# Block sums of a graph layer turned by transposing matmuls, and six buffers of gathered rows instead of seven

## The chip, the cores and the metric

The kernel runs on one core of one Trainium2 chip. A core has five instruction streams that matter here: TensorE (PE in the profile; its loads of stationary operands are listed as PEld), VectorE (DVE), ScalarE (ACT), GpSimd (POOL), and SyncE (SP), beside the queues that carry transfers. The metric is device microseconds from launch to end; lower is better. Three runs of the kernel before gave 4693.23, 4697.88 and 4697.90 us, with a median of 4697.88 us. All arithmetic is float32.

## What is computed

The reference is one message passing layer over a graph of 12500 nodes with 160 features each (64 scalars, and 32 vectors of three components) and 400000 edges, sorted by the node that they end in. Cut to what matters:

```python
h_s = s @ lin1_ws * a / sqrt(64);  h_v = (v @ lin1_wv) * a / sqrt(32)   # per node
w1, w2, w3, w4, w5 = split(silu(edge_scalars @ fc_w1 / 8) @ fc_w2 / 8)  # per edge, 224 wide
es, ev = h_s[src], h_v[src]                                             # gathered rows
e0, e1 = edge_attr[:, :1], edge_attr[:, 1:4]
m_s1 = w1 * es * e0;            m_s2 = w4 * einsum(ev, e1) / 3
m_v1 = (w2 * es) x e1;          m_v2 = w3 * ev * e0
m_v3 = w5 * cross(ev, e1) / 2
agg = segment_sum(concat(m_s1, m_s2), concat(m_v1, m_v2, m_v3); dst) / 4
o = (agg @ lin2) * a            # per node
pre = sc + o                    # sc = (x @ sc_w) * a, the self connection
g = concat(silu(pre_s[:64]), sigmoid(pre_s[64:96]) * pre_v)
out = layernorm(x + g)
```

## The kernel before, in words

**Tiles, steps and blocks.** The edges are cut into 3125 tiles of 128, one edge to a partition. A step handles four tiles, so there are 782 steps; the main loop runs over them and writes the instructions of every engine in the order in which they stand in the program. Nothing reorders them later. Three tiles in a row are a block; two blocks make a pair, and the tiles of a step alternate between the two blocks' places. Since the edges are sorted, the edges of a block end in a window of at most 16 nodes in a row.

**One step.** `gather` (L471) issues four indirect transfers on POOL's queue, one for each tile; each fetches 128 rows of 160 values from a table `h_tab` of node features into a buffer `hg`. These buffers come from the pool `deep`. The third of a step's four gathers has an extra wait, called the pace: it does not start before the last `weights` matmul of three steps earlier is done. `weights` (L546) makes the 224 edge weights of each of the four tiles on PE, into one of two PSUM buffers `pw`. DVE then makes a one-hot matrix of edge against window node (`one_hot`, L609, into a free part of `pw`), the products of weights and gathered rows (`products`, L556 and three times L564) and `sel`, the one-hot matrix times the four edge attributes (L618). Two steps later `sum_up` has PE add up the tiles of a block with `sel` as the stationary operand (L625, into PSUM buffer `pa`): 64 rows (four attributes times 16 nodes) by 416 columns of products for each of the pair's two blocks.

**What a pair's sums go through.** `close` copies a finished `pa` to SBUF as `sa` (ACT, L853): 128 partitions, of which the index is block, attribute, node. `turned` (L641) brings this onto the other axis for two pairs at a time: products on partitions, attribute and node on columns. For each of the four groups of 128 product columns it multiplies a slice of `sa` by those columns of the unit matrix `ident` that select the wanted attributes (three attributes, 96 columns, for two groups; one attribute, 32 columns, for the other two), into a PSUM buffer of the kind `misc`; ACT copies the result into `tt` (L644). When eight pairs or so have gathered in `tt`, `second` multiplies by the second linear map (L654), ACT copies that to `os` (L657), and DVE adds each block's window into the accumulator `acc` of all nodes (L662). One step's hidden layer (L462 on PE, L464 on ACT) is made for every two steps, also through `misc`, of which there are two buffers.

**The nodes' end.** `finish` handles four tiles of 128 nodes at a time: `turn` makes, for a tile's scalars and vectors, the self connection (L709) and then adds the turned piece of `acc` behind it by a product with `ident` (L711), both into one `misc` buffer; tanh, gate, layer norm and the store (L714 to L756) follow.

**What sets the order.** The loop gives each half of a step at most one of the odd jobs: a hidden layer, a turn of sums, a second map, a turn of nodes (`spread_out`). In the last steps the order follows what is ready. DVE, ACT and POOL wait for PE through semaphores; two `pw`, two `pa` and two `misc` buffers and the pool `deep` bound how far one engine runs ahead of another.

A matmul instruction of float32 operands shows as two records in the profile, each with a weight load of its own.

Of the kernel before, what the change touches and what calls it, by code (L numbers as in the profile page):

```python
# [10 lines left out]
F32 = mybir.dt.float32  # L11
# [10 lines left out]
P = 128  # L22
S = 64
V = 32
V3 = 3 * V
# [6 lines left out]
W = 16  # L32
# [17 lines left out]
NPR = 2 * S + 3 * V3  # L50
ROWS = 4 * W
# [10 lines left out]
def gnn_kernel(  # L62
# [21 lines left out]
    nc = tc.nc  # L84
# [10 lines left out]
    consts = ctx.enter_context(tc.tile_pool(name="consts", bufs=1))  # L95
# [111 lines left out]

    ident = consts.tile([P, P], F32, name="ident")
    make_identity(nc, ident)
    iota_i = consts.tile([P, W], I32, name="iota_i")  # L210
    nc.gpsimd.iota(iota_i, pattern=[[1, W]], base=0, channel_multiplier=0)
    eps = consts.tile([P, 1], F32, name="eps")
# [415 lines left out]

    def turned(psum, sas, tt, b, n):

        pt = psum.tile([P, 8, 4, W], F32, name="pt", tag="misc")
        k = n * ROWS
        wanted = ident.rearrange("p (b k w) -> p k b w", b=2, k=4)[:k]
        for m, sa in enumerate(sas):
            plane = 0
            for four in range(4):
                c = min(four * P, NPR - P)
                of = slice(1, 4) if four < 2 else slice(0, 1)
                planes = slice(plane, plane + of.stop - of.start)
                plane = planes.stop  # L640
                nc.tensor.matmul(pt[:, planes, m * n:(m + 1) * n], sa[:k, c:c + P],  # L641
                                 wanted[:, of, :n], start=True, stop=True)
        n *= len(sas)
        nc.scalar.copy(tt[:, :, b:b + n], pt[:, :, :n])  # L644

    def second(pool, psum, tt, nb):
        po = psum.tile([V3, 2, NO, W], F32, name="po", tag="misc")
        for k, to in enumerate("sv"):
            of = [key for key in terms if key[0] == to]
            for n, (_, part, four) in enumerate(of):  # L650
                assert part and four < 2 or not part and four >= 2
                r = slice(P - V if four == 3 else 0, P)
                a = tt[r, four * 3 + part - 1 if part else 4 + four]
                nc.tensor.matmul(po[:, k, :nb], l2[r, terms[to, part, four]], a[:, :nb],  # L654
                                 start=(n == 0), stop=(n == len(of) - 1))
        os = pool.tile([V3, 2, NO, W], F32, name="os", bufs=1)
        nc.scalar.copy(os[:, :, :nb], po[:, :, :nb])  # L657
        return os
# [21 lines left out]
    def finish(fin, psum, t0, nt, p, most=NF, pool=None):  # L680
# [17 lines left out]
        def turn(ks, away=False):  # L698
            if not held:
                held.extend(fin.tile([P, most, *shape], F32, name=name) for name, shape in (  # L700
                    ("g", [V3]), ("y", [D]), ("st", [6]), ("mv", [2]), ("rs", [])))
            g, y = held[:2]
            pp = psum.tile([P, 2, 2, V3], F32, name="pp", tag="misc")
            for k in ks:
                c = (t0 + k) * P
                for m in range(2):
                    if connect:
                        w, a = ((scs, xs), (scv, xv))[m]
                        nc.tensor.matmul(pp[:, k % 2, m], a[:, k * P:(k + 1) * P], w,  # L709
                                         start=True, stop=False)  # L710
                    nc.tensor.matmul(pp[:, k % 2, m], acc[:, m, c:c + P], ident[:V3, :V3],  # L711
                                     start=not connect, stop=True)
            for k in ks:
                nc.scalar.activation(g[:, k], pp[:, k % 2, 0], AF.Tanh, scale=half_at[:, t0 + k:t0 + k + 1])  # L714

            n = len(ks)
            if away:
                pc = fin.tile([P, 2, 2, V3], F32, name="pc", bufs=2)
                nc.scalar.copy(pc[:, :n], pp[:, :n])
                pp = pc  # L720

            def gate():
                k = slice(ks[0], ks[0] + n)
                nc.vector.scalar_tensor_tensor(y[:, k, :S], g[:, k, :S], 1.0, pp[:, :n, 0, :S],
                                               op0=OP.add, op1=OP.mult)
                for k in ks:
                    nc.vector.scalar_tensor_tensor(
                        y[:, k, S:].rearrange("p (c i) -> p i c", i=3),
                        g[:, k, None, S:].to_broadcast([P, 3, V]), 1.0,
                        pp[:, k % 2, 1].rearrange("p (i c) -> p i c", i=3),  # L730
                        op0=OP.add, op1=OP.mult)
                for k in ks:
                    nc.vector.scalar_tensor_tensor(y[:, k], y[:, k], half_at[:, t0 + k:t0 + k + 1],
                                                   xt[:, k], op0=OP.mult, op1=OP.add)

            return gate
# [33 lines left out]
    with tc.tile_pool(  # L770
# [3 lines left out]
    ) as mine, tc.tile_pool(  # L774
        name="late", bufs=2
    ) as late, tc.tile_pool(name="edge", bufs=2) as edge, tc.tile_pool(
        name="deep", bufs=7
    ) as deep, tc.tile_pool(name="banks", bufs=1, space=PSUM) as banks:
        pw_ps = Banks(banks, "pw", Q * 256, 2)
        pa_ps = Banks(banks, "pa", 512, 2)  # L780
# [416 lines left out]
```

## Time and profile before

| what | value |
|---|---|
| median of three runs | 4697.88 us |
| the profiled execution | 4732.17 us |
| its span, first to last instruction | 4730.4 us |
| mean granted TensorE clock | 0.88 |
| PE busy | 4056.1 us (86%), 19977 records |
| POOL busy | 2986.1 us (63%), of which gathers 2955.4 us |
| DVE busy | 2369.7 us (50%) |
| ACT busy | 840.1 us (18%) |
| bytes moved | 412.54 MB, 87 GB/s on average |

The profiled execution is 34 us (0.7%) longer than the median; differences are to be read within one execution. Busy shares are averages over the whole span. An idle time in the profile stands in square brackets behind the instruction that ended it, with the name of what released it; "issue" is idle time that no recorded event explains, and "remote" is a release that the profile could not put down to an instruction just then ending (the page's name for it is "another core or an unknown queue"; here there is only one core). "x4" behind a row counts records that were put together.

### The profile page before, as it was taken

To read this page: it belongs to the slowest core of one execution; us is meant where nothing else is said; L and a number is where in the kernel's file an instruction comes from. 1 tells how busy PE (TensorE), PEld (TensorE's weight loads), DVE (VectorE), ACT (ScalarE), POOL (GpSimd) and SP (SyncE) were. 2 spreads that over 40 slices of the span, in tenths; PEclk is the share of its full clock that TensorE was granted. 3 is DMA by queue.
4 is the path that set the end of the run, shared out by engine and by line. 5 is a ranking of instruction groups with operands and counts; after the bars stand their busy time and mean duration, and the time that the engine had idled before them with its cause. 6 is when DMAs were issued, how large, how long until landed. Compare 5 with 4: busy or idle time off the path is not lost.

```text
span 4730.4 us, 57897 instructions
## 1 busy us (share of the span) xinstructions
PE 4056.1 (86%) x19977; PEld 2153.1 (46%) x19977; DVE 2369.7 (50%) x6410; ACT 840.1 (18%) x1872; POOL 2986.1 (63%) x3172
## 2 busy tenths in 40 slices
PE   5888888888888898888888888888888888888887
PEld 3444444444444444444444444444444444444444
DVE  5544554545544445545455455454554545545454
ACT  1211111111111111111211111111111111111112
POOL 5666666666666666666666666666666666666663
PEclk8888898988998888898898898888898889888898
DMA  6333333333333333333333333333333333333331
GB/s 204 92 77 78 94 86 78 93 78 85 94 77 86 86 84 87 85 85 84 88 85 84 88 85 84 88 85 78 93 85 78 93 77 87 94 77 87 88 83 46
DMA packets 237527, 412.54 MB, mean 87 GB/s; under 512 B 78040, under 2 KB 160961, under 8 KB 237093
## 3 DMA queue, kind: packets, MB, share of 16 engines
q0 software_dynamic: 152960, 266.64, 21.5%
q1 hardware_dynamic: 83668, 141.96, 12.4%
q8 instruction: 160, 2.62, 0.2%
q14 instruction: 145, 1.19, 0.1%
q10 hardware_dynamic: 594, 0.13, 0.0%
HBM read 392.49 MB, written 16.00 MB: 86 GB/s over the span
## 4 chain that ended last, share of the span: by engine, by line
PE 55%; DVE 15%; another core or an unknown queue 14%; issue 11%; POOL 3%; DMA 2%; ACT 0%; DVEq 0%; SPq 0%; POOLq 0%; ACTq 0%
PE pa L625 20%; PE pw L546 13%; DVE pr L564 8%; PE misc L641 7%; PE misc L462 6%; PE misc L654 6%; POOL hg L471 3%; DVE sel L618 2%; PE misc L711 2%; DVE pr L556 1%; PE misc L709 1%; DVE pw L609 1%; DVE acc L662 1%; DMA hg<-h_tab,idx 1%
## 5 line engine op out<-in xcount | busy, mean ns | idle before, releaser
L471 POOL DMA_INDIRECT hg<-h_tab,idx x3125 | 2955.4, 946 | 1682.1 <-issue 823.6
L625 PE MATMUL pa<-pr,sel 128*64 128x416 f32 x6250 | 1610.4, 593 | 167.5 <-issue 164.2
L609 DVE TENSOR_TENSOR pw<-rel,iota 128x64 f32<-128x64 int16 x782 | 179.1, 229 | 2199.7 <-remote 1374.9
L564 DVE TENSOR_TENSOR pr<-pw,hg 128x384 f32<-128x384 f32 x2346 | 1152.2, 546 | 0.0
L546 PE MATMUL pw<-w,hid 64*128 64x224 f32 x6250 | 954.4, 407 | 171.6 <-issue 66.4
L546 PEld LDWEIGHTS pw<-w,hid 64*128 64x128 f32 x6250 | 609.0, 205 | 818.5 <-issue 536.8
L625 PEld LDWEIGHTS pa<-pr,sel 128*64 128x64 f32 x6250 | 447.8, 149 | 1047.0 <-issue 1011.3
L641 PE MATMUL misc<-ident,sa 128*128 128x96 f32 (+1 forms) x4168 | 613.2, 297 | 111.5 <-issue 107.6
L641 PEld LDWEIGHTS misc<-ident,sa 128*128 128x128 f32 x4168 | 568.8, 213 | 203.1 <-issue 196.6
L556 DVE TENSOR_TENSOR pr<-pw,hg 128x512 f32<-128x512 f32 x782 | 540.0, 691 | 29.1 <-DVE pw L609 1.5
L462 PE MATMUL misc<-es,w 128*128 128x512 f32 (+1 forms) x784 | 464.2, 672 | 38.7 <-DVE rel L424 19.6
L644 ACT COPY tt<-misc 128x512 f32<-128x512 f32 (+1 forms) x263 | 152.9, 581 | 1697.8 <-remote 982.8
L464 ACT ACTIVATE hid<-misc 128x512 f32<-128x512 f32 x392 | 234.9, 599 | 916.8 <-remote 469.8
L853 ACT COPY sa<-pa 128x416 f32<-128x416 f32 x521 | 263.6, 506 | 548.8 <-PE pw L546 207.4
L654 PE MATMUL misc<-tt,l 128*96 128x256 f32 (+5 forms) x1496 | 357.9, 386 | 3.2 <-issue 2.6
L618 DVE TENSOR_TENSOR sel<-pw,eas 128x256 f32<-128x256 f32 x782 | 321.5, 411 | 0.1
L654 PEld LDWEIGHTS misc<-tt,l 128*96 128x96 f32 (+1 forms) x1496 | 224.4, 165 | 131.0 <-issue 72.9
L662 DVE TENSOR_TENSOR acc<-acc,os 96x32 f32 x1042 | 193.5, 186 | 83.5 <-PE misc L711 32.4
L711 PE MATMUL misc<-ident,acc 96*128 96x96 f32 x392 | 116.6, 393 | 135.5 <-DVE acc L662 118.3
L462 PEld LDWEIGHTS misc<-es,w 128*128 128x128 f32 x784 | 124.3, 198 | 163.5 <-issue 147.0
L711 PEld LDWEIGHTS misc<-ident,acc 96*128 96x128 f32 x392 | 87.2, 276 | 152.0 <-DVE acc L662 124.1
L657 ACT COPY os<-misc 96x512 f32<-96x512 f32 (+2 forms) x68 | 38.3, 563 | 477.4 <-PE pw L546 134.3
(93 smaller groups left out, 695.2 us busy)
## 6 DMA issues: line engine op xcount, KB each, us to landing
es<-in_es_t_dram SPq DMA_DIRECT2D x258, 384.0 KB
hg<-h_tab,idx POOLq DMA_INDIRECT x3125
h_tab<-ht POOLq DMA_DIRECT2D x24, 320.0 KB
xt<-in_x_dram SPq DMA_DIRECT2D x23, 320.0 KB
out_dram<-y SPq DMA_DIRECT2D x23, 320.0 KB
xv<-in_xv_t_dram SPq DMA_DIRECT2D x23, 192.0 KB
eat<-in_ea_dram SPq DMA_DIRECT2D x41, 96.0 KB
xw<-in_xs_t_dram SPq DMA_DIRECT2D x6, 512.0 KB
```

The costliest lines, as they stand in the source:

```text
L462: nc.tensor.matmul(ph[:k, c], w1[:k, :k], es[:k, t0 * P + c0 * P:t0 * P + c1 * P], start=True, stop=True)
L471: got = nc.gpsimd.indirect_dma_start(out=hg[:, t, :], out_offset=None, in_=h_tab, in_offset=bass.IndirectOffsetOnAxis(ap=i, axis=0))
L546: weighed.append(nc.tensor.matmul(pw[:, t, :NWT], hid[r, c * P:(c + 1) * P], w2[r], start=True, stop=True).ins.name)
L556: nc.vector.tensor_mul(two, pw[:, :n, :2 * S].rearrange("p t (k c) -> p t k c", k=2), hg[:, :n, None, :S].to_broadcast([P, n, 2, S]))
L564: nc.vector.tensor_mul(pr[:, :n, first:first + V3].rearrange("p t (i c) -> p t i c", i=3), pw[:, :n, None, 2 * S + k * V:2 * S + (k + 1) * ...
L618: nc.vector.tensor_mul(sel[:, :n], oh[:, :, None, :].to_broadcast([P, n, 4, W]), by_slot(tiles[0][0])[:, u:u + n, :, None].to_broadcast([P ...
L625: summed.append(nc.tensor.matmul(pa[half * ROWS:(half + 1) * ROWS, :NPR], sel[:, t].rearrange("p k w -> p (k w)"), pr, start=start, stop=s ...
L641: nc.tensor.matmul(pt[:, planes, m * n:(m + 1) * n], sa[:k, c:c + P], wanted[:, of, :n], start=True, stop=True)
L654: nc.tensor.matmul(po[:, k, :nb], l2[r, terms[to, part, four]], a[:, :nb], start=(n == 0), stop=(n == len(of) - 1))
L662: nc.vector.tensor_add(window, window, os[:, :, b])
L711: nc.tensor.matmul(pp[:, k % 2, m], acc[:, m, c:c + P], ident[:V3, :V3], start=not connect, stop=True)
L853: nc.scalar.copy(sa, pas.pop(j)[:, :NPR])
```

## The change

Three things change.

1. **Turning the sums of pairs.** A second constant `first_last` is made at the start (two copies on DVE): the unit matrix with its columns in another order, so that the first attribute comes last. `turned` now uses transposing matmuls of 128 columns (`is_transpose`), by `ident` or by `first_last`, for seven of the eight products of two pairs; each writes all four attributes, and the planes that are not wanted are overwritten by a later write. The eighth is an ordinary product of 32 columns. Where only one pair is turned, four transposing matmuls do it. The planes of `tt` stand in another order, which the copy and `second` follow. In the whole program 1826 transposing and 258 ordinary matmuls take the place of 2084 ordinary ones.
2. **Turning the nodes' sums.** In `turn` the piece of `acc` is transposed first (196 transposing matmuls in the place of 196 ordinary ones), and the self connection is added behind it.
3. **Buffers.** The pool `deep` of gathered rows has six buffers instead of seven.

```diff
+    first_last = consts.tile([P, P], F32, name="first_last")
+    by_kind = ident.rearrange("p (b k w) -> p k b w", b=2, k=4)
+    ordered = first_last.rearrange("p (k b w) -> p k b w", b=2, k=4)
+    nc.vector.tensor_copy(ordered[:, :3], by_kind[:, 1:])
+    nc.vector.tensor_copy(ordered[:, 3:], by_kind[:, :1])
...
     def turned(psum, sas, tt, b, n):
 
-        pt = psum.tile([P, 8, 4, W], F32, name="pt", tag="misc")
-        k = n * ROWS
-        wanted = ident.rearrange("p (b k w) -> p k b w", b=2, k=4)[:k]
-        for m, sa in enumerate(sas):
-            plane = 0
-            for four in range(4):
-                c = min(four * P, NPR - P)
-                of = slice(1, 4) if four < 2 else slice(0, 1)
-                planes = slice(plane, plane + of.stop - of.start)
-                plane = planes.stop
-                nc.tensor.matmul(pt[:, planes, m * n:(m + 1) * n], sa[:k, c:c + P],
-                                 wanted[:, of, :n], start=True, stop=True)
-        n *= len(sas)
-        nc.scalar.copy(tt[:, :, b:b + n], pt[:, :, :n])
+        pt = psum.tile([P, 512], F32, name="pt", tag="misc")
+        k, w = n * ROWS, n * W
+        fours = {four: min(four * P, NPR - P) for four in range(4)}
+        by_first = ident.rearrange("p (b k w) -> p k b w", b=2, k=4)[:k, :, :n]
+        by_last = first_last.rearrange("p (k b w) -> p k b w", b=2, k=4)[:k, :, :n]
+        writes = [(0, 2, 0, by_first), (0, 3, 1, by_first), (0, 0, 2, by_last), (0, 1, 5, by_last)]
+        if len(sas) == 2:
+            writes = [(1, 1, 12, by_first), (1, 0, 9, by_first), (1, 3, 6, by_last), *writes,
+                      (1, 2, 8, by_first[:, :1])]
+        for m, four, at_p, moving in writes:
+            of = sas[m][:k, fours[four]:fours[four] + P]
+            kinds = moving.shape[1]
+            to = pt[:, at_p * w:(at_p + kinds) * w]
+            nc.tensor.matmul(to.rearrange("p (k b w) -> p k b w", k=kinds, b=n), of, moving,
+                             start=True, stop=True, is_transpose=kinds == 4)
+        m = len(sas)
+        nc.scalar.copy(
+            tt[:, :, b:b + n * m].rearrange("c f (m b) w -> c m f (b w)", m=m),
+            pt[:, :8 * w * m].rearrange("c (m f x) -> c m f x", m=m, f=8))
...
-                a = tt[r, four * 3 + part - 1 if part else 4 + four]
+                a = tt[r, 2 + four * 3 + part - 1 if part else four - 2]
...
                 for m in range(2):
+                    nc.tensor.matmul(pp[:, k % 2, m], acc[:, m, c:c + P], ident[:V3, :V3],
+                                     start=True, stop=not connect, is_transpose=True)
                     if connect:
                         w, a = ((scs, xs), (scv, xv))[m]
                         nc.tensor.matmul(pp[:, k % 2, m], a[:, k * P:(k + 1) * P], w,
-                                         start=True, stop=False)
-                    nc.tensor.matmul(pp[:, k % 2, m], acc[:, m, c:c + P], ident[:V3, :V3],
-                                     start=not connect, stop=True)
+                                         start=False, stop=True)
...
-        name="deep", bufs=7
+        name="deep", bufs=6
```

The lines of the file move down by five to ten: the matmuls of L641 become L649, and those of L546, L625, L711 and L709 become L551, L630, L717 and L721.

On PE the turn of two pairs in the middle of the program, where `sa` are the sums of two pairs and `pa` the next pair's sums, stands like this before:

```order
L641 MATMUL misc_513<-ident,sa 128x3x32 [waits Activation_49]
L641 MATMUL misc_513<-ident,sa 128x3x32
L641 MATMUL misc_513<-ident,sa 128x32 x2
L641 MATMUL misc_513<-ident,sa 128x3x32 x2
L641 MATMUL misc_513<-ident,sa 128x32 x2
L625 MATMUL pa_511<-pr,sel 64x416 x4
```

and, at the same place, like this now:

```order
L649 MATMUL misc_516<-ident,sa 128x128 [waits Activation_49]
L649 MATMUL misc_516<-ident,sa 128x128
L649 MATMUL misc_516<-first_last,sa 128x128
L649 MATMUL misc_516<-ident,sa 128x128 x2
L649 MATMUL misc_516<-first_last,sa 128x128 x2
L649 MATMUL misc_516<-ident,sa 128x32
L630 MATMUL pa_514<-pr,sel 64x416 x4
```

The group keeps its place and its single wait for ACT; seven of its eight matmuls are now of 128 columns. The place of the group among PE's other work has not moved.

On PE the first turn of two tiles of nodes, where `xs`, `xv` are the nodes' features and `acc` the accumulator that DVE adds to, stands like this before:

```order
L709 MATMUL misc_513<-scs,xs_3098 128x96 [waits DMAHW6_49,Activation_49]
L711 MATMUL misc_513<-ident,acc 128x96 [waits DVE_49]
L709 MATMUL misc_513<-scv,xv_3099 128x96 [waits DMAHW7_49]
L711 MATMUL misc_513<-ident,acc 128x96
L709 MATMUL misc_513<-scs,xs_3098 128x96
L711 MATMUL misc_513<-ident,acc 128x96
```

and like this now:

```order
L717 MATMUL misc_516<-ident,acc 128x96 [waits DVE_49,Activation_49]
L721 MATMUL misc_516<-scs,xs_3101 128x96 [waits DMAHW6_49]
L717 MATMUL misc_516<-ident,acc 128x96
L721 MATMUL misc_516<-scv,xv_3102 128x96 [waits DMAHW7_49]
L717 MATMUL misc_516<-ident,acc 128x96
L721 MATMUL misc_516<-scs,xs_3101 128x96
```

The wait for DVE's additions has moved ahead of the first self connection, which stood in front of it before.

## The prediction

> **What bounds the kernel now.** The page first: busy times, the chain of waits, the costliest groups.
>
> ```profile
> PE 4056.1 (86%) x19977; PEld 2153.1 (46%) x19977; DVE 2369.7 (50%) x6410; ACT 840.1 (18%) x1872; POOL 2986.1 (63%) x3172
> ...
> PE 55%; DVE 15%; another core or an unknown queue 14%; issue 11%; POOL 3%; DMA 2%; ACT 0%; DVEq 0%; SPq 0%; POOLq 0%; ACTq 0%
> ...
> L471 POOL DMA_INDIRECT hg<-h_tab,idx x3125 | 2955.4, 946 | 1682.1 <-issue 823.6
> ...
> L641 PE MATMUL misc<-ident,sa 128*128 128x96 f32 (+1 forms) x4168 | 613.2, 297 | 111.5 <-issue 107.6
> ...
> L711 PE MATMUL misc<-ident,acc 96*128 96x96 f32 x392 | 116.6, 393 | 135.5 <-DVE acc L662 118.3
> ```
>
> PE is 86% busy and more than half of the chain, and the change cuts PE's records, so at first sight it hits the bound. But 14% of the chain are releases that nobody is named for. The gathers' own line and POOL's list of waits (total us, times, longest) come next.
>
> ```profile
> L471 POOL DMA_INDIRECT hg<-h_tab,idx x3125: 940/946/1105, 51.8 to 4683.7; - x196
> ```
>
> ```profile
> POOL hg L471 <- issue: 823.6, 2663, 3.6
> POOL hg L471 <- remote: 514.8, 232, 3.5
> POOL hg L471 <- PE pw L546: 186.1, 80, 13.7
> POOL hg L471 <- PE misc L462: 57.5, 30, 3.5
> POOL hg L471 <- PE pa L625: 47.6, 21, 3.5
> ```
>
> The gathers fill 4632 us of the span (51.8 to 4683.7), that is 5.92 us for each of 782 steps. An unhindered gather takes 0.946 us and 823.6/2663 = 0.31 us before the next, so four take 5.02 us and 782 steps some 3930 us. The other 700 us are stalls: the four lower rows are 806 us over 363 times, 2.22 us each, of which 0.31 is there anyway. They stand at the third gather, whose pace waits for L546 of three steps earlier. What ends such a stall is seen in the timeline (start, duration, what):
>
> ```profile
> 1995.66 1.44 PE L546 MATMUL pw<-w,hid 64*128 64x224 f32 x8
> ...
> 1999.46 0.94 POOL L471 DMA_INDIRECT hg<-h_tab,idx  x1 [0.30 <-issue]
> ...
> 2000.49 0.35 PE L709 MATMUL misc<-scs,xs 64*128 64x96 f32 x2
> 2000.71 0.95 POOL L471 DMA_INDIRECT hg<-h_tab,idx  x1 [0.30 <-issue]
> 2003.46 0.23 DVE L609 TENSOR_TENSOR pw<-rel,iota 128x64 f32<-128x64 int16 x1 [5.82 <-remote]
> ...
> 2003.50 0.60 ACT L464 ACTIVATE hid<-misc 128x512 f32<-128x512 f32 x1 [4.49 <-remote]
> 2003.70 0.94 POOL L471 DMA_INDIRECT hg<-h_tab,idx  x1 [2.04 <-remote]
> ```
>
> PE has done with the needed L546 at 1997.1 by the profile. DVE, ACT and POOL, which wait for three different matmuls, all go on within 0.24 us of each other at 2003.5, 1.8 us after the last gather left POOL. I read this as a hold: while gathers flow, PE's completions reach the others late, and only a pause of the gathers lets them through together. That is inferred from the coincidence, not shown. It makes the stall a fixed pause once every two or three steps, and not a measure of PE's work. Three neighbouring stretches from stall to stall test that (PE, PEld, DVE, ACT, POOL busy with records, granted clock, DMA):
>
> ```profile
> 1281.63:1293.39 11.76, 10.64 (x51) 4.16 (x50) 5.78 (x16) 1.69 (x4) 7.56 (x8) 1.00 0.21 57
> 1293.39:1311.00 17.61, 12.24 (x48) 6.86 (x50) 8.71 (x25) 1.72 (x4) 11.35 (x12) 0.79 0.46 108
> 1311.00:1322.75 11.75, 11.75 (x60) 6.80 (x56) 5.29 (x13) 2.16 (x5) 7.56 (x8) 0.88 0.22 58
> ```
>
> 51 and 60 PE records take the same 11.75 us at clocks of 1.00 and 0.88. The middle stretch is one of three steps, 17.61 us, 5.87 a step instead of 5.88. So PE's count does not set the step; the number of gathers and one pause do.
>
> **The change part by part.** Records: 2084 matmuls of L641 are 4168 records, 2 each. The only transposition in the trace is one record:
>
> ```profile
> L796 PE MATMUL misc<-ident,far x1: 372/372/372, 217.5 to 217.5; 128*1 128x128 f32 x1
> ```
>
> So 1826 transposes save 1826 records, and 196 of L711 another 196: 2022 of 19977, 10%. Two pairs go from 16 records to 9, one pair from 8 to 4.
>
> The price of a record in a stream, and of the nodes' records:
>
> ```profile
> 2017.90 1.97 PE L641 MATMUL misc<-ident,sa 128*128 128x96 f32 x16
> ```
>
> ```profile
> 2006.52 0.74 PE L711 MATMUL misc<-ident,acc 96*128 96x96 f32 x2 [5.67 <-DVE acc L662]
> 2007.05 0.64 PE L709 MATMUL misc<-scv,xv 96*128 96x96 f32 x2
> ```
>
> 16 records of 96 and 32 columns follow each other at 1.97/16 = 0.12 us. A transposing record has 128 columns and the same load, so it lies between 0.12 us and the lone 0.372 us of L796; I take 0.15, near the row of the same 128-wide load in a stream. A group is then 9 x 0.15 = 1.35 instead of 1.97 us; at 0.372 it would be 3.35, longer than before. L711 falls by one of the four records, (2007.48 less 2006.52)/4 = 0.24 us, of each half tile. On PE alone that is 260 groups x 0.62 us + 196 x 0.24 us = 208 us, none of which is worth anything where the pause sets the step.
>
> The Trainium skill (TensorE: Matmul & The Clock Gate, Part 4: PE-mode transpose) gives about 275 ns for a transposition inside a kernel, of a 16-bit type; by that a group would be 9 x 0.275 = 2.5 us, longer than the 1.97 us of the row, the tail's 34 records 9.4 us, no gain, and the sum -20 instead of -23 us.
>
> What does count is, first, the stretch of three steps. Its stall is longer:
>
> ```profile
> 1310.58 0.58 ACT L644 COPY tt<-misc 128x512 f32<-128x512 f32 x1 [15.89 <-remote]
> ...
> 1311.00 0.94 POOL L471 DMA_INDIRECT hg<-h_tab,idx  x1 [2.91 <-remote]
> ```
>
> 2.91 instead of 2.04 us. ACT's copy of the turned sums comes through 0.42 us ahead of POOL, so L641's 16 records stand in front of the awaited L546 when the held completions come through. If those 0.87 us are the passing of 16 records, seven fewer save 0.87 x 7/16 = 0.38 us. Of 335 whole stretches of two or three steps in the list of L471's starts 51 are of three steps; the first and the last:
>
> ```profile
> 155.59:173.16 17.57, 11.35 (x13) 0.87 0.45 108
> 4632.53:4650.23 17.70, 11.35 (x12) 0.83 0.21 57
> ```
>
> 51 x 0.38 = 19 us; at least 0 (if something else makes it longer), at most 51 x 0.87 = 44.
>
> Second, the tail. After the last gathers nothing is held and PE is followed at once:
>
> ```profile
> 4674.85 4.32 PE L641 MATMUL misc<-ident,sa 128*128 128x96 f32 x24
> 4681.25 0.94 POOL L471 DMA_INDIRECT hg<-h_tab,idx  x1 [9.59 <-PE pw L546]
> 4693.28 1.97 PE L641 MATMUL misc<-ident,sa 128*128 128x96 f32 x16
> 4696.33 0.46 PE L711 MATMUL misc<-ident,acc 96*128 96x96 f32 x2
> 4699.94 1.08 PE L641 MATMUL misc<-ident,sa 128*128 128x96 f32 x8
> 4703.80 1.00 PE L641 MATMUL misc<-ident,sa 128*128 128x96 f32 x8
> 4707.64 1.08 PE L641 MATMUL misc<-ident,sa 128*128 128x96 f32 x8 [0.60 <-ACT sa L853]
> 4713.82 3.73 PE L711 MATMUL misc<-ident,acc 96*128 96x96 f32 x16 [1.28 <-DVE acc L662]
> ...
> 4717.45 0.29 DVE L724 SCALAR_TENSOR_TENSOR y<-g,misc 128x128 f32<-128x128 f32 x1 [2.09 <-DMA out_dram<-y]
> ```
>
> The five groups of L641 are 9.45 us for 64 records; 34 remain. At the old price per record that saves 9.45 x 30/64 = 4.4 us, at 0.15 us, a quarter dearer, about 3.2. The four pairs of L711 from 4696.33 lose half of 4 x 0.43, 0.8 us; the last group at 4713.82 is covered by the store that L724 waits for. Together -4; bounds -6 and, at 0.372, +4.
>
> Parts that I cost at nothing. Six buffers: a step's first gather then needs the products of six steps earlier instead of seven. The third gather of the step before had already waited for L546 of four steps before this one, and that matmul could write its `pw` (two in turn) only after the products and `sel` of six steps before; the order is implied. The two copies at the start are some 0.3 us each (128x128 on DVE, as L724's 0.29) and stand ahead of an idle 1.34 us:
>
> ```profile
> 4.98 0.29 DVE L298 TENSOR_TENSOR l1v<-wv,sides 128x128 f32<-128x128 f32 x1 [1.34 <-DMA wv<-in_lin_wv_dram]
> ```
>
> without that cover +0.6. ACT copies as many elements as before, with runs of 32 instead of 64 (L644, 0.58 us): 0 to +0.1 us each, and ACT is 18% busy. In a turn of nodes the first L709 pair (0.35 us at 2000.49) now stands behind the wait for `acc`: at most +0.35 us in each of 49 turns (392 records of L711, 8 a turn), 17 us, if PE had to be prompt there; the 5.67 us that PE waited at 2006.52 came out of a hold, and PE was ahead, so 0.
>
> Sum: -19 - 4 = -23 us, on the execution profiled (4732.2 to 4709). That execution lies 34 us above the median; on the median it gives 4698 - 23 = 4675 us.
>
> **The rivals.** More is gained. If fewer records let the gathers run longer between pauses, all stretches become three steps with a stall of 2.91 - 0.38 = 2.53: (3 x 5.02 + 2.22)/3 = 5.76 us a step instead of 5.92, -125 us, 4573. If PE itself set the pace, all 208 us would go: 4490. For it: the chain, PE's 86%, and PE standing idle for "issue" within these stretches. Against it: 51 and 60 records in equal time.
>
> It gets slower. PE's lead is what keeps the stall at 2 us; where PE is late, the third gather waits for real work, as at 4681.25 behind 24 records of L641: 9.59 us, 7.55 more than at 2003.70. The mechanism would be the clock.
>
> ```profile
> core 0: 4730.4 us, clock 0.880
> ```
>
> PE at full clock needs 4056 x 0.88 = 3570 us, so a mean clock below 3570/4632 = 0.77 makes PE the bound; locally 0.79 (the stretch at 1293.39) was still covered. If transposing leaves PE fewer full-clock stretches, each new late one costs up to 7.55 us: three undo the gain, ten give -23 + 75 = +52 us, 4750.
>
> The same section of the Trainium skill says that transposing matmuls do not count as PE work for the clock gate, which speaks for this case; the trace, with one transposition in it, can't show it.
>
> It does nothing that can be told: the long stall isn't made by L641's records, or the transposing record is as slow as L796, and only the tail remains, -6 to +4 us: 4697.
>
> **How the numbers follow.** About 0.2% (9 us) is what a measurement of this kernel can tell from no change. The hold stays and the gain is small, -10 to -60 us: 0.48. A gain of 60 to 250 us: 0.14. Within 9 us: 0.12. Slower: 0.26, mostly up to 4750. So faster 0.62, same 0.12, slower 0.26. The predicted time is the likeliest case's, 4675; its own range is 4638 to 4688. The range 4560 to 4735 takes in the three-step rival and half of the slower case's distance; it leaves out a PE-bound gain (0.07) and the slower half of the slower case (0.1).
>
> **What would show it.** L649 with 2342 records (1826 + 2 x 258) and PE's count some 2000 lower: the records. Gathers from about 52 to some 4660 us, POOL's stalls still near 2 us and mostly of two steps: the hold. Stalls after three steps near 2.5 instead of 2.9 us: the first term. The tail from the last gather to the end 3 to 5 us shorter: the second. The granted clock tells the slower rival: 0.88 or more denies it, 0.8 or less with stalls of 5 us and more confirms it. The prediction is wrong if gathers stop stalling (then PE's completions were not held by them) or if PE's lead is lost.

## The result and the profile after

The changed kernel takes 4664.12 us (median; 4659.28 to 4664.60), the kernel before 4695.56 us beside it (4689.13 to 4697.90): 31 us less, a ratio of 0.9933 with a 95% interval of 0.9916 to 0.9950. The two profiled executions differ by more, 4732.17 against 4659.28 us, since the one of before lay above its kernel's other times and the one of after below. So 73 us lie between the two profiles, and 41 of them are differences between executions of one kernel (37 us on the side of before, 5 us on that of after). What follows reads the pattern from the profiles and the size from the medians, and a sum taken from the two profiles is not the worth of the change.

The page of the changed kernel, the lines that answer to those shown of before:

```profile
PE 3852.9 (83%) x17955; PEld 1891.7 (41%) x17955; DVE 2369.7 (51%) x6412; ACT 840.2 (18%) x1872; POOL 2995.5 (64%) x3172
...
PE 63%; issue 12%; another core or an unknown queue 10%; DVE 9%; DMA 2%; POOL 2%; ACT 1%; DVEq 0%; SPq 0%; ACTq 0%; POOLq 0%
...
L476 POOL DMA_INDIRECT hg<-h_tab,idx x3125 | 2964.8, 949 | 1601.1 <-issue 824.7
...
L649 PE MATMUL misc<-ident,sa 128*128 128x128 f32 (+1 forms) x1558 | 311.3, 290 | 76.6 <-ACT sa L863 42.3
...
L649 PE MATMUL misc<-first_last,sa 128*128 128x128 f32 x784 | 188.8, 297 | 4.3 <-issue 4.2
L717 PE MATMUL misc<-ident,acc 96*128 96x96 f32 x196 | 64.0, 332 | 95.7 <-DVE pw L614 68.3
```

PE has 17955 records, 2022 fewer, as counted: 1558 + 784 = 2342 of L649 in the place of 4168, 196 of L717 in the place of 392. PE is 203 us less busy.

The gathers' line and POOL's waits (total us, times, longest):

```profile
L476 POOL DMA_INDIRECT hg<-h_tab,idx x3125: 942/949/1125, 51.3 to 4613.1; - x196
```

```profile
POOL hg L476 <- remote: 443.6, 187, 3.1
POOL hg L476 <- PE pw L551: 146.7, 81, 7.2
POOL hg L476 <- PE misc L467: 56.5, 36, 4.1
POOL hg L476 <- PE misc L649: 47.5, 26, 3.0
POOL hg L476 <- PE pa L630: 22.9, 15, 2.8
POOL hg L476 <- PE misc L664: 20.8, 8, 2.7
```

The gathers now fill 4561.8 us instead of 4632, 70 us of the 73 between the two profiles. From the last gather's start to the end it is 44.4 us instead of 46.7; that is the tail. The stalls remain, but there are fewer. In the list of the gathers' starts the next one is more than 1.6 us away (1.25 is the normal interval) 327 times here and 374 times before, and what goes beyond 1.25 us adds up to 644 instead of 725 us. A gather itself takes 949 ns instead of 946, which costs 9 us.

Stretches from stall to stall at the same place as those shown of before (us; PE, PEld, DVE, ACT, POOL busy with records; clock; DMA):

```profile
1270.85:1288.26 17.41, 14.88 (x66) 6.44 (x63) 8.71 (x24) 2.96 (x7) 11.38 (x13) 0.87 0.46 109
1288.26:1299.93 11.67, 11.67 (x55) 6.78 (x55) 5.20 (x12) 1.76 (x5) 7.58 (x9) 0.85 0.22 58
1299.93:1317.29 17.36, 13.33 (x71) 6.40 (x69) 8.46 (x22) 3.45 (x12) 11.39 (x13) 0.97 0.43 102
1317.29:1334.61 17.32, 14.98 (x68) 6.62 (x67) 8.71 (x24) 2.09 (x5) 11.38 (x12) 0.80 0.21 58
```

What was one three-step stretch among two-step ones is now the common kind. In the list of the gathers' starts, from 150 us on, there are 150 stretches of three steps and 129 of two, where the kernel before has 51 and 282. Both kinds are shorter in this profile. The time beyond 1.25 us for each gather is on average 2.41 us in a stretch of three steps (2.59 before) and 1.60 us in one of two (1.82 before). A step costs 5.80 us in either kind now, where it cost 5.86 and 5.91.

### The profile page after: what moved, and what is told of

It is laid out like the page before. It is cut to its first block, busy times and chain, and to the rows that moved or that the text cites. A ratio compares the mean times of both kernels' runs of the same rounds, so it can differ in the third digit from the quotient of the medians.

```text
span 4657.5 us, 53879 instructions
## 1 busy us (share of the span) xinstructions
PE 3852.9 (83%) x17955; PEld 1891.7 (41%) x17955; DVE 2369.7 (51%) x6412; ACT 840.2 (18%) x1872; POOL 2995.5 (64%) x3172
## 4 chain that ended last, share of the span: by engine, by line
PE 63%; issue 12%; another core or an unknown queue 10%; DVE 9%; DMA 2%; POOL 2%; ACT 1%; DVEq 0%; SPq 0%; ACTq 0%; POOLq 0%
PE pa L630 23%; PE pw L551 17%; PE misc L664 8%; PE misc L467 7%; PE misc L649 6%; DVE pr L569 5%; POOL hg L476 2%; PE misc L721 2%; DMA hg<-h_tab,idx 1%; DVE sel L623 1%; PE misc L717 1%; DVE pr L561 1%; DVE pw L614 1%; DMA xz<-in_xv_t_dram 1%
## 5 line engine op out<-in xcount | busy, mean ns | idle before, releaser
L630 PE MATMUL pa<-pr,sel 128*64 128x416 f32 x6250 | 1546.6, 585 | 122.8 <-issue 118.5
L551 PE MATMUL pw<-w,hid 64*128 64x224 f32 x6250 | 1050.7, 408 | 382.9 <-issue 257.7
L551 PEld LDWEIGHTS pw<-w,hid 64*128 64x128 f32 x6250 | 644.2, 203 | 1078.8 <-issue 742.1
L630 PEld LDWEIGHTS pa<-pr,sel 128*64 128x64 f32 x6250 | 444.4, 149 | 971.3 <-issue 924.5
L467 PE MATMUL misc<-es,w 128*128 128x512 f32 (+1 forms) x784 | 491.3, 709 | 30.5 <-DVE rel L429 19.6
L664 PE MATMUL misc<-tt,l 128*96 128x256 f32 (+5 forms) x1496 | 400.3, 411 | 42.8 <-issue 40.6
L649 PE MATMUL misc<-ident,sa 128*128 128x128 f32 (+1 forms) x1558 | 311.3, 290 | 76.6 <-ACT sa L863 42.3
L664 PEld LDWEIGHTS misc<-tt,l 128*96 128x96 f32 (+1 forms) x1496 | 241.9, 176 | 194.9 <-issue 125.9
L649 PEld LDWEIGHTS misc<-ident,sa 128*128 128x128 f32 x1558 | 218.5, 173 | 162.2 <-issue 100.5
L649 PE MATMUL misc<-first_last,sa 128*128 128x128 f32 x784 | 188.8, 297 | 4.3 <-issue 4.2
L717 PE MATMUL misc<-ident,acc 96*128 96x96 f32 x196 | 64.0, 332 | 95.7 <-DVE pw L614 68.3
```

What stands on the lines that cost most here:

```text
L467: nc.tensor.matmul(ph[:k, c], w1[:k, :k], es[:k, t0 * P + c0 * P:t0 * P + c1 * P], start=True, stop=True)
L551: weighed.append(nc.tensor.matmul(pw[:, t, :NWT], hid[r, c * P:(c + 1) * P], w2[r], start=True, stop=True).ins.name)
L630: summed.append(nc.tensor.matmul(pa[half * ROWS:(half + 1) * ROWS, :NPR], sel[:, t].rearrange("p k w -> p (k w)"), pr, start=start, stop=s ...
L649: nc.tensor.matmul(to.rearrange("p (k b w) -> p k b w", k=kinds, b=n), of, moving, start=True, stop=True, is_transpose=kinds == 4)
```

## The experiments

The theory was that where gathers flow PE's completions reach the other engines late, that a pause of the gathers lets them through, and that the records to be passed in it set how long the stretches and the stalls are. The rivals were that PE's time sets the pace, and that the buffers or the nodes' sums carry a part.

**Parts of the change by themselves.** The kernel before with six buffers:

```diff
-        name="deep", bufs=7
+        name="deep", bufs=6
```

> The kernel before with six buffers of gathered rows instead of seven, and nothing else. Theory (the order of products, pw and pace implies the free buffer): 0, ratio 0.999 to 1.001, POOL's stalls in two-step stretches as before. Rival (part of the gain comes from the gathers being held closer to PE by fewer buffers): 5 us or more faster, with more stretches of three steps. A loss of 5 us or more would say that the seventh buffer was used.

The kernel before with the nodes' turn alone:

```diff
+                    nc.tensor.matmul(pp[:, k % 2, m], acc[:, m, c:c + P], ident[:V3, :V3],
+                                     start=True, stop=not connect, is_transpose=True)
                     if connect:
                         w, a = ((scs, xs), (scv, xv))[m]
                         nc.tensor.matmul(pp[:, k % 2, m], a[:, k * P:(k + 1) * P], w,
-                                         start=True, stop=False)
-                    nc.tensor.matmul(pp[:, k % 2, m], acc[:, m, c:c + P], ident[:V3, :V3],
-                                     start=not connect, stop=True)
+                                         start=False, stop=True)
```

> The kernel before with the turn of the nodes' sums alone (196 one-record transposes ahead of the self connection). Theory: 196 records fewer of 19977, the tail 1 us shorter, hardly another stretch of three steps: 0 to -3 us. Rival (the wait for the accumulator, now ahead of the whole group, is paid in each of 49 turns): +5 to +17 us.

The changed kernel with the diff just shown taken back, so that the pairs' sums alone are turned by transposes:

> The changed kernel with the nodes' sums turned as before: the turn of the pairs' sums (with six buffers) alone. Theory: it carries nearly all of the gain, -25 to -31 us against the kernel before, and the stretches of three steps are as frequent as in the changed kernel (about 150, where the kernel before has 51). Rival (the three parts add up from equal pieces): -10 to -20 us.

The changed kernel with small extra matmuls:

```diff
+        for _ in range(2 * len(sas)):
+            nc.tensor.matmul(pt[:32, :32], sas[-1][:k, :32], ident[:k, :32], start=True, stop=True)
         for m, four, at_p, moving in writes:
```

> The changed kernel with four small extra matmuls (32 x 32, two records each) at the head of each turn of two pairs, two at that of one pair: 17 and 8 records where the changed kernel has 9 and 4 and the kernel before 16 and 8. Their results are overwritten. Theory (the number of PE records that must pass between two pauses decides whether a stretch has two or three steps): back to the kernel before, 4685 to 4697 us, with some 50 to 80 stretches of three steps. Rival (PE's time decides; the small records are short): most of the gain stays, 4664 to 4675 us, with over 120 stretches of three steps.

The kernel before took 4002.37 us beside these four, not 4697. The ratios were 1.0000 (0.9991 to 1.0009), 1.0004 (0.9995 to 1.0013), 0.9994 (0.9985 to 1.0003) and 1.0003 (0.9994 to 1.0012): no part, and not the turn of the pairs' sums either, moves the time there. The kernel with six buffers, otherwise the kernel before, shows why. Its gathers' line, then POOL's waits:

```profile
L471 POOL DMA_INDIRECT hg<-h_tab,idx x3125: 942/946/1096, 52.7 to 3962.5; - x196
```

```profile
POOL hg L471 <- issue: 794.6, 2609, 0.3
POOL hg L471 <- DMA hg<-h_tab,idx: 42.0, 138, 0.3
POOL hg L471 <- DVE pw L609: 20.4, 67, 0.3
POOL hg L471 <- PE pw L546: 19.2, 63, 0.3
```

In these rows no wait is longer than 0.3 us, the usual gap between two gathers. All 3125 gathers run without a stall, in 3909.8 us, near the 3930 us that the prediction gave for unhindered gathers. And DVE's idle time before the one-hot matrix has no "remote" in it. The largest row of the kernel before, profiled at 4732 us, and then that of the kernel with six buffers:

```profile
DVE pw L609 <- remote: 1374.9, 247, 18.6
```

```profile
DVE pw L609 <- PE pw L546: 521.7, 344, 5.7
```

With each one-hot matrix set beside the last L546 record of its own step, DVE went on less than 0.2 us after the end of that record in 342 of the 367 cases in which it waited there. In the profile of the kernel before, 417 of 493 such waits ended more than 0.6 us after it, 350 of them 3 to 10 us. So the late completions are no property of the kernel's instructions: the kernel before itself ran here without the stalls' time. These four runs tell nothing of the parts under late completions.

**More PE time, the same records.** The eighth matmul of a two-pair turn made 512 columns wide (it overwrites the other results):

```diff
         for m, four, at_p, moving in writes:
+            if moving.shape[1] == 1:
+                nc.tensor.matmul(pt.rearrange("p (a b) -> p a b", a=4), sas[m][:k, fours[four]:fours[four] + P],
+                                 ident[:k, None, :].to_broadcast([k, 4, P]), start=True, stop=True)
+                continue
```

> The changed kernel with the one ordinary matmul of each turn of two pairs made 512 columns wide instead of 32 (it then overwrites the other results, so the sums of blocks that reach the output are not the reference's): the same instructions and records, but about 1 us more PE time in each of 258 turns, more than the change took away. Theory (records count, PE's time does not while PE is ahead): within 10 us of the changed kernel, 4660 to 4675 us. Rival (PE's time sets the pace): the gain is gone and more, 4700 us or above; if PE bounded everything, 4664 + 260 = 4920 us.

Measured beside a kernel before of 4002.8 us: ratio 0.9997 (0.9987 to 1.0006). Where completions come at once, PE's time has no effect either. The expectation was written for the other condition, and this run does not test it.

**Fewer gathers.** Two of four gathers of each step left out, in the kernel before and in the changed one; all four tiles take the first tile's rows:

```diff
         for t, i in enumerate(idx):
+            if t % 2:
+                continue
...
-            hg[:, :n, None, :S].to_broadcast([P, n, 2, S]))
+            hg[:, :1, None, :S].to_broadcast([P, n, 2, S]))
...
-                hg[:, :n, S:].rearrange("p t (i c) -> p t i c", i=3))
+                hg[:, :1, S:].rearrange("p t (i c) -> p t i c", i=3).to_broadcast([P, n, 3, V]))
```

> The kernel before with two of four gathers left out of each step (the products of all four tiles use the first tile's rows, so the result is not the reference's): POOL then has 2.5 us of work in a step. Theory (the pauses are the gathers' and PE's completions come through when no gather runs): the long idle times before the one-hot matrix that end together for DVE, ACT and POOL become rare, and PE sets the pace: 3600 to 4300 us. Rival (the stalls come from PE being late in the full kernel too): the time hardly falls, 4600 us or more.

> The changed kernel with the same two gathers of a step left out. Theory: where PE sets the pace the whole of PE's saving shows, 120 to 250 us below the kernel before with the same gathers left out, several times the 31 us of the full kernel. Rival (what is gained does not depend on who sets the pace): 20 to 50 us below.

3422.7 and 3192.1 us (ratios 0.8551 and 0.7976 to the kernel before at 4002.8). The first is below its range of 3600 to 4300 us; completions came at once in these runs, so they show what PE's time is worth where PE sets the pace, and nothing of what gathers do to late completions. The difference of the two is 230.6 us, within the 120 to 250 of the theory. The chain of waits of the two, before and after, and their clocks:

```profile
PE 96%; DVE 1%; issue 1%; POOL 1%; DMA 0%; ACT 0%; ACTq 0%; DVEq 0%; POOLq 0%
```

```profile
PE 96%; DVE 2%; issue 1%; DMA 1%; POOL 1%; ACT 0%; ACTq 0%; DVEq 0%; POOLq 0%
```

```profile
core 0: 3420.2 us, clock 0.992
```

```profile
core 0: 3187.9 us, clock 0.993
```

With PE as the bound the change is worth 230.6 us, 6.7%. A two-pair group in the second of these kernels:

```profile
1008.35 0.44 PE L651 MATMUL misc<-ident,sa 128*128 128x128 f32 x2
1008.62 0.27 PE L651 MATMUL misc<-first_last,sa 128*128 128x128 f32 x1
1008.73 0.38 PE L651 MATMUL misc<-ident,sa 128*128 128x128 f32 x2
1008.95 0.38 PE L651 MATMUL misc<-first_last,sa 128*128 128x128 f32 x2
1009.17 0.31 PE L651 MATMUL misc<-ident,sa 128*128 128x32 f32 x2
1009.40 1.62 PE L632 MATMUL pa<-pr,sel 128*64 128x416 f32 x8
```

Nine records take 1009.40 - 1008.35 = 1.05 us to the next work, 0.117 us each; the sixteen of before, from 2017.90 to the next work, take 1.90 us:

```profile
2019.80 0.92 PE L625 MATMUL pa<-pr,sel 128*64 128x416 f32 x4
```

257 groups by 0.85 us are 218 us of the 230.6.

**A looser pace, and the changed kernel itself.**

```diff
-                    deep, [index(t) for t, _, _ in tiles], {2: weighed_by[n - 3] if n >= 7 else None})
+                    deep, [index(t) for t, _, _ in tiles], {2: weighed_by[n - 4] if n >= 8 else None})
```

> The changed kernel with the third gather's pace waiting for the weights of four steps earlier instead of three. Theory (a stall is one fixed pause of about 2 us plus what must pass in it, and comes when the pace catches up with the completions that are held): stretches of three and four steps take the place of those of two and three, with stalls some 0.5 us longer; 4620 to 4665 us. Rival (the stall is PE's lateness): the stalls shrink with each step of slack, and the time goes towards the gathers' own 4000 us.

> The changed kernel itself, beside the kernel before on the same chip. In the runs of the eight kernels so far the kernel before took 4002 us, and no completion of PE was held there. Theory (the gain comes through the stalls after held completions): where the kernel before takes some 4002 us the changed one takes 3999 to 4003 us, as much as the tail gives; where it takes some 4697 us, 4655 to 4672 us, with about 150 stretches of three steps. Rival (the gain is PE's time and shows anywhere): 20 us or more below also at 4002 us.

The first gave 0.9997 (0.9987 to 1.0006) beside 4002.8 us: there is no stall to loosen, so neither side of its expectation was tested. The changed kernel itself gave 0.9999 (0.9990 to 1.0009) beside 4002.05 us, within what the theory said for that case. Its gathers:

```profile
L476 POOL DMA_INDIRECT hg<-h_tab,idx x3125: 942/946/1117, 52.8 to 3962.5; - x196
```

The last one starts when that of the kernel with six buffers starts, at 3962.5; the span is 4000.3 us instead of 4002.4. These 2.1 us of tail are all that the two traces show of the change where completions come at once, and the medians (4001.74 beside 4002.05 us) can't tell them from nothing.

The changed kernel was thus profiled in both conditions, and the traces also record when a semaphore is updated, that is, when a completion reaches the other engines. In the execution of 4002.10 us, 2163 of the 2165 recorded updates of PE's semaphore come within 0.04 us of the end of a matmul that makes one. In that of 4659.28 us it is 400 of 1997. There 50% of the updates fall into pauses of more than 0.6 us between two gathers, which take 16% of the gathers' time; of the matmul ends 10% fall there. So the late completions themselves, and that half of them come through in a sixth of the time, the gathers' pauses, are on record and not only inferred from engines that restart together. For DVE the trace can't tell: only 1991 of its 3815 updates are recorded there, against 3794 in the other.

**No pace.**

```diff
-                    deep, [index(t) for t, _, _ in tiles], {2: weighed_by[n - 3] if n >= 7 else None})
+                    deep, [index(t) for t, _, _ in tiles])
```

> The changed kernel without the pace: the third gather no longer waits for the weights of three steps earlier (only for its buffer and its index). On a chip where PE's completions are seen at once (the kernel before at 4002 us) the theory expects nothing, 3999 to 4003 us, since no gather waits there for the pace. On one where they are seen late (the kernel before near 4697 us) the stalls move to a step's first gather, which waits for its buffer, with longer stretches and longer stalls: within 40 us of the changed kernel. Rival (the pace itself makes the stalls): the gathers run through there too, some 4000 us.

This time the kernel before took 4737.14 us, on a chip listed under the same number as the one that had given 4002.05. The kernel without the pace took 5132.47 us, a ratio of 1.0837 (1.0807 to 1.0868). Both expectations missed: the gathers do not run through, and the loss, 395 us, is ten times what the theory allowed. (The changed kernel itself was not run beside it.) The timeline shows what takes the pace's place:

```profile
2011.32 0.53 PE L551 MATMUL pw<-w,hid 64*128 64x224 f32 x1 [1.60 <-issue]
...
2012.96 0.95 POOL L476 DMA_INDIRECT hg<-h_tab,idx  x1 [0.30 <-issue]
...
2013.44 0.53 PE L551 MATMUL pw<-w,hid 64*128 64x224 f32 x1 [1.59 <-issue]
...
2014.85 0.53 PE L551 MATMUL pw<-w,hid 64*128 64x224 f32 x1 [0.88 <-issue]
...
2016.25 0.53 PE L551 MATMUL pw<-w,hid 64*128 64x224 f32 x1 [0.87 <-issue]
...
2016.95 1.12 PE L551 MATMUL pw<-w,hid 64*128 64x224 f32 x4 [0.18 <-issue]
2017.05 0.23 DVE L614 TENSOR_TENSOR pw<-rel,iota 128x64 f32<-128x64 int16 x1 [7.62 <-remote]
2017.15 0.58 ACT L652 COPY tt<-misc 128x512 f32<-128x512 f32 x1 [10.15 <-remote]
...
2019.67 0.94 POOL L476 DMA_INDIRECT hg<-h_tab,idx  x1 [5.77 <-DVE pr L569]
```

The gathers run on, mostly for three or four steps, until they need a buffer that DVE must free. By then even PE starts only one matmul every 1.4 to 2.1 us, with no reason in the profile; 3.1 us after the last gather left POOL, the four records after 2016.95 follow each other and DVE and ACT are released together. POOL then has to wait for DVE's work besides, 5.77 us here. That the pace helps where completions are late is measured; that it does so by a short pause in time, before so much is held, is the likeliest reading of this stretch.

**Records against PE's time, with late completions.** The wide and the small matmuls again:

> The changed kernel with the wide ordinary matmul once more (records as in the changed kernel, PE time above that of the kernel before), in the hope of a chip where PE's completions are seen late. There (the kernel before near 4700 us): if the count of records carries the gain, a ratio to the kernel before of 0.990 to 0.996, as the changed kernel's, and 130 to 170 stretches of three steps; if PE's time carries it, 1.000 or above, and some 50 such stretches or fewer. Where the kernel before takes 4002 us: 1.000, as before, and nothing learned.

> The changed kernel with the small extra matmuls once more (records as in the kernel before, PE time between the two). Where the kernel before takes some 4700 us: if the count of records carries the gain, a ratio of 0.998 to 1.003 and 50 to 80 stretches of three steps; if PE's time carries it, 0.993 to 0.998 and over 100. Where the kernel before takes 4002 us: 1.000, and nothing learned.

The kernel before took 4740.39 us, so both tell something. Stretches of the kernel with the small matmuls, at the same place:

```profile
1278.76:1290.53 11.77, 10.56 (x52) 4.40 (x50) 5.78 (x16) 1.69 (x4) 7.56 (x9) 1.00 0.22 56
1290.53:1308.18 17.65, 11.27 (x50) 6.17 (x51) 8.77 (x24) 1.72 (x4) 11.34 (x12) 0.77 0.49 108
1308.18:1319.98 11.80, 11.80 (x68) 7.03 (x67) 5.30 (x13) 2.17 (x5) 7.56 (x8) 0.91 0.23 56
```

and of the one with the wide matmul:

```profile
1287.53:1305.17 17.64, 14.58 (x64) 6.10 (x63) 8.76 (x25) 2.49 (x6) 11.40 (x12) 0.89 0.48 107
1305.17:1316.90 11.73, 11.73 (x55) 6.58 (x55) 5.21 (x13) 2.14 (x6) 7.58 (x8) 0.89 0.23 58
```

The first reads like the kernel before, stretch by stretch. The changed kernel was not run on this occasion; its row comes from the result above, beside 4695.56 us, and that of before from the profile of 4732 us. Over the whole program, with the time of a two-pair group from its first start to the next work at full clock:

| kernel | records of a group | time of a group | stretches of 3 and 2 steps | mean time beyond the gathers in them | ratio to the kernel before (95%) |
|---|---|---|---|---|---|
| before | 16 | 1.90 us | 51, 282 | 2.59, 1.82 us | 1 |
| changed | 9 | 1.06 us | 150, 129 | 2.41, 1.60 us | 0.9933 (0.9916 to 0.9950) |
| wide | 9 | 1.77 us | 111, 163 | 2.64, 1.64 us | 0.9953 (0.9936 to 0.9969) |
| small | 17 | 1.43 us | 56, 280 | 2.66, 1.84 us | 0.9975 (0.9964 to 0.9985) |

The wide matmul was to have cost 1 us a group and cost 0.71, so its PE time is just below that of before, not above. The two kernels of this occasion can be compared directly: the wide one spends more time in a group and has fewer records, and at 4717.19 us it is 10.6 us faster than the small one at 4727.78. So what is gained here does not go by PE's time alone, and the count of three-step stretches goes with the records, 111 against 56. Beside the changed kernel's ratio, the wide one keeps some two thirds of the gain with 85% of the saved time given back, and the small one a third with over half of the saved time kept; but these shares compare two occasions.

Neither expectation holds in full. The wide kernel's ratio came as for records, its 111 three-step stretches fell short of 130; the small one's stretches came as for records, its ratio as for time. With as few records as the changed kernel, the wide one has the long three-step stalls of before (2.64 us), and it has 65 stretches of a single step where the kernel before has 25 and the changed one 27. So PE's time has a share too. How large it is, three ratios with such intervals don't say. Each record comes with a weight load of its own, and these runs don't tell the two apart.

## Why the prediction was right

The forecast was -23 us, to 4675 us; it came out at -31 us, 4664 us, in the likeliest case's own range. What bounds the kernel was read rightly. That the number came so near is in part luck: the terms of the sum came out smaller than forecast, and effects that it had put at nothing or into a rival made up for them.

- **The stalls are pauses after late completions, not PE's work.** Held. The stalls stay at the third gather, 318 of 327. The seven kernels with all their gathers that ran with completions at once have no stalls, last gathers that start within 2 us of each other (3960.8 to 3962.5 us) whatever PE does, and no gain clear of noise. That completions are late, and that half of them come through in the gathers' pauses, is shown by the semaphore's updates. That the flow of gathers is what makes them late is still inferred: the same flow ran without any delay at other times, and why was not found. The pauses are not of a fixed length either; they differ with the kernel (the table above).
- **The long stall, -19 us.** Too large, and its mechanism is not shown. A three-step stretch lost 0.18 us instead of 0.38, which makes 9 us of 51 of them. The two-step ones, which were given nothing, lost 0.22 us each, 62 us for the 282 of before. The two terms add up to about the 70 us by which the gathers of the two profiles differ, more than twice the 31 us of the medians; so part of the shortening belongs to the executions and not to the change, and one profile of each doesn't say how much. That a three-step stall shortens because fewer records pass in it would have to show in the wide kernel too, which has seven records fewer and stalls of 2.64 us.
- **More three-step stretches**, which the prediction put into a rival at up to -125 us, while its own case had the stalls "mostly of two steps". They came, 150 for 51. At the step costs of before (5.86 and 5.91 us) some 300 steps more in such stretches are worth about 13 us; in the changed kernel a step costs 5.80 us in both kinds, near the 5.76 that the rival had for all.
- **The price of a transposing record, 0.15 us.** Transposing records start 0.11 us after one another (1008.73 to 1008.95 is two of them), nine records take 0.117 us each, and a group saves 0.85 us instead of 0.62. The upper price, 0.372 us, is how long one record lasts and not how soon the next can follow: here a transposing record lasts 273 ns, and in the stream they overlap. On PE alone the change is worth 230.6 us, where 208 were worked out.
- **The tail, -4 us.** 2.1 to 2.3 us in the profiles.
- **Six buffers, nodes' turn at nothing.** 1.0000 and 1.0004 where completions come at once; with late completions they were not tried by themselves, so a part of the 31 us may be theirs.
- **The slower rival, by the clock.** The mean clock went from 0.880 to 0.870, just under the 0.88 that was to deny this rival. But gathers that wait 5 us or more are two before and two after, and the late third gather near the end waits 7.22 us instead of 9.59. The Trainium skill (TensorE: Matmul & The Clock Gate, Part 4: PE-mode transpose) says that transposes do not count as PE work for the clock gate in the way that other matmuls do; where PE was 98% busy, the clock was 0.993 with some 2000 transposes among 17955 records and 0.992 without, so at such a share nothing of that shows here. Its 275 ns inside a kernel, for a 16-bit type, is the time that one transposition lasts; the trace agrees, with 273 ns for 128x128 float32. The prediction multiplied it by the number of records, as if they did not overlap.

```profile
L649 PE MATMUL misc<-first_last,sa x784: 269/273/472, 105.3 to 4635.5; 128*128 128x128 f32 x196
```

## What to carry to other kernels

When several engines that wait for different instructions go on in the same instant, ask what had just stopped, before the busiest engine is taken for the bound: this change is worth 230 us where PE is the bound, 31 us where completions come late, and at most some 2 us where neither is so. Leaving out part of the other engine's work (here half of the gathers) prices a saving on an engine that is covered. And one program can have two regimes that differ by 17%, so the kernel before belongs beside every run.

## What the runs showed of the hardware

The same kernel took 4002 us in some runs and 4695 to 4740 us in others, on chips of which one was listed under the same number both times. The profiles name the difference. Where the kernel takes 4002 us the updates of PE's semaphore come within 0.04 us of the end of the matmul (2163 of 2165 in the changed kernel); where it takes 4659 us, 400 of 1997 do, and half of them come in the gathers' pauses. What brings it about was not found.

A weight load ahead of a transposing matmul takes 141 ns (median) where that of the ordinary matmul by an operand of the same 128x128 shape takes 192 ns; after and before:

```profile
L649 PEld LDWEIGHTS misc<-first_last,sa x784: 138/141/231, 105.2 to 4635.4; 128*128 128x128 f32 x196
```

```profile
L641 PEld LDWEIGHTS misc<-ident,sa x4168: 186/192/338, 108.5 to 4708.4; 128*128 128x128 f32 x199
```
